# Two attention layers on one core: other engines for the matrix sums between the phases, and own timetables for the first and last pairs

## The chip, the cores and the metric

The kernel runs on one core of a Trainium2 chip. A core has a matrix engine (TensorE, "PE" in the profile), three engines for elementwise work (VectorE or DVE, ScalarE or ACT, GpSimd or POOL) and SyncE (SP), which in this kernel only issues transfers (DMA). Every engine works through its own list of instructions strictly in order; semaphores make one wait for another. The metric is the time of one execution on the device in microseconds (us), the median of several runs.

## The reference

The input `x` has 128 graphs of 64 nodes with 768 features, in float32, and `adj` holds which nodes are joined. Two layers follow, each with a residual and a normalisation over the features. The first is a graph attention of 12 heads of 64 with a gate, the second an ordinary masked attention of 6 heads of 128.

```python
# layer 0
h = einsum('bnd,ade->bane', x, W);  th = tanh(h)
attn = einsum(th, w_src) + swapaxes(einsum(th, w_dst), 2, 3)
attn = softmax(where(adj, leaky(attn, 0.2), -999))
f = elu(einsum('banm,bame->bane', attn, h) + b)
g = sigmoid(x @ H_w.T + H_b)
x = layernorm(x + g * f + (1 - g) * x)
# layer 1
q, k, v = x @ Wq + bq, x @ Wk + bk, x @ Wv + bv          # 6 heads of 128
ctx = softmax(q k^T / sqrt(128) + where(adj, 0, -9e15)) v
x = layernorm(x + ctx @ Wf + bf)
```

## The kernel before

**Tiles and phases.** The 8192 rows are 64 tiles of 128 (two graphs each), 32 pairs of tiles and 16 quads of two pairs. Phase a runs layer 0 pair by pair, and the values v of layer 1 two pairs behind; it writes x after layer 0 (`x1_there`), its transposed blocks (`ops_there`) and v (`v_there`) to the chip's memory. Phase b runs layer 1 quad by quad: queries and keys of three heads at a time (`q_0_0`, `k_0_0`, `q_0_1`, ...), a slab of attention for these, and the output product of the quad before.

**Products by sums.** All large matrix products follow schemes with fewer multiplications (of the Strassen and Winograd kind): sums of blocks are formed first, the products of sums are computed on TensorE, and their results are added up on the other engines. `by_token` (L409) does the two tiles of a pair by two halves of the columns in 7 products of 3 matmuls of 128x384, called P1, P6, P5, P2, P7, P3, P4 in this order; a pair has three such runs, `hidden` (h), `gate` (g) and `value` (v). `by_feature` (L520) and `output` (L1230) have 15 products of two matmuls of 128x256. For these the weights need sums too: a matrix of 18 blocks of 128x256 becomes 15 operands, by 15 sums of blocks (L341 on POOL, or L378, the helper `plus`, on VectorE) and two negated blocks (L344, on ScalarE).

**The border.** Wq and Wk are loaded into the places of layer 0's matrices while the last pair is at work (L328, 18 loads each of half a block). The first queries and keys of quad 0, `q_0_0` and `k_0_0`, are computed by `plain` (L496) from the raw matrices, so that the sums are needed only for `q_0_1` and `k_0_1`. Before, wq's sums run on POOL and wk's on VectorE. `load_third` (L464) loads the operands of quad 0 and `sums_of_quad` (L474, on POOL) makes their sums. The order on TensorE is: h and g of the last pair (p = 31), value(29), plain q, value(30), plain k, value(31), then phase b with `q_0_1` and `k_0_1`.

**Attention of a tile in phase a.** `attend` has 33 small steps on all engines. Those that the texts below speak of: L755 multiplies tanh(h) by the target weights; SP stores the sums (L763) and loads them back, spread over all rows (`bc_e`, L766); L779 adds the mask to them; L805 and twice L378 (`qk`, `th_d`) make the scores; ScalarE takes the exponential (L814); L819 sorts the halves of each number for a transpose by DMA (L823); L826 puts the transposed weights into `bc_e`; 24 small matmuls make the means (`f_all`, L835); L847/L848 divide them, L857 to L865 make the gated sum, L879 normalises, L887 and L891 turn the rows into the blocks for layer 1. L775/L776 sum the sources, L740 loads the tile's rows of x.

**Reads of the products.** L626 (h, P1, on ScalarE), L630, L633, L641, L645, L649 read h's products from PSUM; L670 to L686 those of the gate, L703 to L723 those of v, all in the `dense` buffers of six banks: a product waits until the one six before it has been read.

**Who decides the order.** A planner (`Beat`) writes each engine's list. Its clock counts beats: one beat is one product of `by_token`, a pair has 21. Every step of `attend` is put at the beat `begin + key` of a table: `FIRST_KEYS` for pairs 0 and 1, `KEYS` for all others, one row for each of the two tiles of a pair. Within a beat the earlier key goes first. The table moves nothing on the chip by itself; it decides what stands before what on each engine. All transfers stand in one list on SP, in the order in which the planner comes to them, and each waits for the eighth before it to have landed. `beat.start(line, after)` begins a chain of steps `after + 0.7` beats from now. In phase b the chain `slab` (s_ps, L1080; L1091 to L1105 on VectorE; c_ps, L1151) starts 0.25 beats after the keys; the reads of the output product (L1243, into `y`) are on VectorE too.

Of the kernel before, what the change touches and what calls it, by code (L numbers as in the profile page):

```python
# [49 lines left out]
ALU = mybir.AluOpType  # L50
# [115 lines left out]
FIRST_KEYS = (  # L166
    (
        (
            7.30, 8.42, 11.50, 8.19, 12.19, 14.50, 14.76, 14.89, 11.54, 17.99, 15.15,
            15.17, 15.52, 18.41, 19.39, 21.69, 23.72, 26.15, 26.31, 27.17, 27.75, 28.71,  # L170
            29.26, 30.33, 33.18, 34.13, 35.27, 35.86, 39.11, 15.41, 21.02, 22.80, 9.19,
        ),
        (
            8.80, 9.00, 13.78, 11.92, 12.01, 15.72, 15.83, 15.87, 13.82, 23.32, 19.70,
            20.58, 21.10, 23.37, 24.39, 24.67, 27.57, 29.73, 30.19, 32.26, 32.47, 32.59,
            33.08, 33.10, 34.28, 35.83, 36.62, 36.84, 39.74, 14.57, 15.41, 22.26, 5.31,
        ),
    ),
    (
        (  # L180
            7.11, 7.74, 9.44, 11.47, 13.51, 13.72, 14.07, 14.80, 16.89, 20.73, 14.98,
            16.33, 17.32, 18.31, 18.71, 20.99, 23.30, 25.33, 26.19, 26.22, 27.77, 27.77,
            28.33, 28.46, 28.97, 30.32, 34.83, 35.25, 39.50, 14.82, 25.50, 27.55, 9.19,
        ),
        (
            9.59, 9.73, 12.30, 13.34, 15.30, 17.56, 18.57, 18.68, 19.34, 24.26, 19.97,
            20.09, 21.15, 22.78, 23.21, 23.90, 26.80, 29.76, 30.49, 31.63, 32.60, 32.89,
            33.74, 34.77, 35.36, 36.41, 36.90, 37.00, 38.50, 16.23, 18.47, 20.43, 5.31,
        ),
    ),  # L190
)

SUMS = (42.40, 42.75, 43.18)
X_BLOCKS = (14.97, 20.25, 20.39)
MASKS = 7.19


FIRST_X_BLOCKS = {1: (2.01, 18.22, 19.86), 2: (17.02, 30.55, 37.15)}
GATE_SUMS = (4.29, 5.74, 7.17, 10.09)
ONE_MORE, VALUE_SUMS = 7.66, 21.30  # L200


class Beat:
# [46 lines left out]
def two_layers(  # L250
# [21 lines left out]
    nc = tc.nc  # L272
    n_tiles = x.shape[0] // P
    n_quads = n_tiles // 4
    n_pairs = n_tiles // 2
    beat = Beat()
# [42 lines left out]
    def thirds(w, name, engine, gap, blocks):  # L319

        t = fifteen(name)
        for k in range(3):
            for m in range(3):
                to = t[:, 3 * k + m]
                if len(blocks.shape) == 6:
                    to = to.rearrange("p c (r e) -> p c r e", r=2)
                    for c in range(2):
                        nc.sync.dma_start(to[:, c], blocks[k, m][:, c])  # L328
                        yield gap
                else:  # L330
                    nc.sync.dma_start(to, blocks[k, m])
                    yield gap
        ready[f"{name}_raw"] = t
        yield 3
        while not ready.get(f"{name}_used", True):
            yield 1
        for to, a, b, op in W_SUMS:
            if engine is nc.vector:
                plus(t[:, to], t[:, a], t[:, b], op)
            else:  # L340
                engine.tensor_tensor(t[:, to], t[:, a], t[:, b], op)  # L341
            yield gap
        for to in NEGATED:
            nc.scalar.mul(t[:, to], t[:, to], -1.0)  # L344
            yield gap
        ready[f"{name}_sb"] = t

# [5 lines left out]
    def by_head(w, name, engine, gap):  # L353

        yield from thirds(w, name, engine, gap, w.rearrange("(k c p) (r n e) -> k n p c r e", k=3, c=2, r=2, n=3))
# [97 lines left out]
    ready, dense = {}, []  # L453
# [90 lines left out]
    def phase_a(pa, ps_a, dst_pool):  # L544
# [67 lines left out]
        def hidden(p, A, B):  # L612
            u = {}

            def h_of(S, m):
                return S["h"][:, 6 * m : 6 * m + 6, 0:E0]

            def th_of(S, m):
                return heads(S["th"][:, m * HALF : (m + 1) * HALF], 6)

            def half_done(S, m):
                beat.soon(lambda: nc.scalar.activation(th_of(S, m), h_of(S, m), AF.Tanh))

            def p1(ps):
                u[1] = part(f"h1_{p}")
                nc.scalar.copy(u[1], ps)  # L626

            def p6(ps):
                u[2] = part(f"h2_{p}")
                nc.vector.tensor_tensor(u[2], u[1], ps, ALU.add)  # L630

            def p2(ps):
                nc.scalar.copy(h_of(A, 0), heads(ps, 6))  # L633
                nc.scalar.activation(th_of(A, 0), heads(ps, 6), AF.Tanh)

            def p5(ps):
                u[3] = part(f"h3_{p}")
                nc.vector.tensor_tensor(u[3], u[1], ps, ALU.add)

            def p7(ps):  # L640
                nc.vector.tensor_tensor(h_of(B, 1), heads(u[3], 6), heads(ps, 6), ALU.add)  # L641
                half_done(B, 1)

            def p4(ps):
                nc.vector.tensor_tensor(h_of(B, 0), heads(u[1], 6), heads(ps, 6), ALU.add)  # L645
                nc.scalar.activation(th_of(B, 0), h_of(B, 0), AF.Tanh)

            def p3(ps):
                nc.vector.tensor_tensor(h_of(A, 1), heads(u[2], 6), heads(ps, 6), ALU.add)  # L649
                nc.scalar.activation(th_of(A, 1), h_of(A, 1), AF.Tanh)  # L650

            by_token(f"h_{p}_", blocks[p], w0_sb, dict(P1=p1, P2=p2, P3=p3, P4=p4, P5=p5, P6=p6, P7=p7))


# [73 lines left out]
        def attend(S, begin):  # L728
            t, p, side, h, th = S["t"], S["p"], S["side"], S["h"], S["th"]
# [166 lines left out]
                means, divided, below, unit, gated, summed, measured, power_of, normal, part_rows,  # L896
                turn_rows, rows, tanh_of_gate, rest_of_gate, rest_of_x, rows_in,
            ]
            for step, key in zip(steps, (FIRST_KEYS[p] if p < 2 else KEYS)[side]):
                beat.at(begin + key, step)  # L900


        def sums_of_pair(p, begin):
            xo, so = x1_at(p), x1_sums
            b = [xo[:, i] for i in range(4)]
            x1_blocks[p] = b + [so[:, i] for i in range(4)]

            def first():
                plus(so[:, 0], b[2], b[3])
                plus(so[:, 1], so[:, 0], b[0], ALU.subtract)  # L910

            def last():
                nc.gpsimd.tensor_tensor(so[:, 2], b[0], b[2], ALU.subtract)
                nc.gpsimd.tensor_tensor(so[:, 3], b[1], so[:, 1], ALU.subtract)

            def away():
                there = ops_there[p // 2][:, p % 2].rearrange("p m c t -> p (m c) t")
                nc.sync.dma_start(there, xo.rearrange("p k c t -> p (k c) t"))

            for work, key in zip((first, last, away), SUMS):  # L920
                beat.at(begin + key, work)

        x1_blocks = {}
# [23 lines left out]
        def first_blocks():  # L947
            for k in (3, 4, 5, 0, 1, 2):
                load_third(0, f"A{k}")
                yield 8 if k == 5 else 0.5  # L950

        period = 3 * len(TURNS)
        for p in range(n_pairs):
            ta, tb = tiles_of(p)
            A = {"t": ta, "p": p, "side": 0}
            B = {"t": tb, "p": p, "side": 1}
            begin = p * period
            for side, S in enumerate((A, B)):
                S.update(h=h_of_tile[(2 * p + side) % 3], th=th_d[side], g=gates[side])
            masks(p, A, B, begin)  # L960
            for S in (A, B):
                attend(S, begin)
            sums_of_pair(p, begin)
            if p + 1 < n_pairs:
                line = x_blocks(p + 1)
                for key in [k - begin for k in FIRST_X_BLOCKS.get(p + 1, ())] or X_BLOCKS:
                    beat.at(begin + key, lambda line=line: next(line, None))
            beat.until(lambda: beat.now == begin)
            if p + 1 == n_pairs:
                ready["wq_used"] = ready["wk_used"] = False  # L970
                beat.start(first_blocks(), 4)
                beat.start(by_head(wq, "wq", nc.gpsimd, 0.3), 7)
                beat.start(by_head(wk, "wk", nc.vector, 0.5), 18)
                beat.start(sums_of_quad(0), 21)
            hidden(p, A, B)
            gate(p, A, B)
            blocks.pop(p)
            if p > 1:
                value(p - 2)
# [1 line left out]
        raw = quads[0].setdefault("raw", set())  # L981
        beat.until(lambda: "wq_raw" in ready and len(raw) == 6)
        plain("q_0_0_", ready["wq_raw"], 0, bq_sb, qk[:, 0])
        ready["wq_used"] = True
        value(n_pairs - 2)
        beat.until(lambda: "wk_raw" in ready)
        plain("k_0_0_", ready["wk_raw"], 0, bk_sb, qk[:, 1])
        ready["wk_used"] = ready["raw_used"] = True
        beat.until(lambda: beat.now > begin + SUMS[1])
        value(n_pairs - 1)  # L990
        beat.drain()

# [12 lines left out]
    def phase_b(pb, ps_b):  # L1005
# [263 lines left out]
        for q in range(n_quads):  # L1269
# [17 lines left out]
                beat.start(operands(before, 1), 6 if final else 0)  # L1287
            beat.until(lambda: "wk_sb" in ready)
            keys(q, 1, None if final else (lambda name: load_third(q + 1, name)))
            beat.start(slab(Q, 1), 0.25)  # L1290
            if final:
                beat.start(rows_of(Q, 0))
                give(0)
# [65 lines left out]
```

## Time and profile before

| what | value |
|---|---|
| median of 3 runs | 2843.06 us (2843.0 to 2844.84) |
| the profiled execution | 2841.36 us |
| its span, from first to last instruction | 2839.6 us |
| TensorE busy | 2777.5 us, 98% of the span |
| VectorE, ScalarE, GpSimd busy | 74%, 49%, 46% |
| mean granted TensorE clock | 0.996 of full speed |
| TensorE busy from 0 to 100 us | 74.51 us |
| TensorE busy from 1300 to 1400, 1400 to 1500 us | 93.21, 95.13 us |

The profile is one execution. Its parts give each engine's busy time, the longest groups of instructions by line of the kernel (L409 is line 409), and for each engine the waits: on which line it waited, for how long in all, how often, and the longest. Lines of the timeline begin with the start in us and the length; a bracket at the end holds the time the engine stood idle before and what released it. Phase a takes the time up to about 1446 us, phase b the rest.

### The profile page before, as it was taken

How to read it: one execution, taken by the hardware profiler on the slowest of the kernel's cores; microseconds unless marked ns; L12 is line 12 of the kernel's file. 1: busy time of each engine (PE TensorE's matmuls, PEld its weight loads, DVE VectorE, ACT ScalarE, POOL GpSimd, SP SyncE). 2: the span in 40 equal slices, each digit the busy share in tenths (PEclk: the TensorE clock that was granted, in tenths of full speed). 3: DMA queues.
4: the chain of work that ended last, by engine and by line, in shares of the span. 5: the costliest groups of instructions: out<-in, count | busy, mean ns of one | idle time of the engine just before them, and what ended most of it. 6: DMA issues, size and time to landing. Idle time of an engine off the chain costs nothing.

```text
span 2839.6 us, 43938 instructions
## 1 busy us (share of the span) xinstructions
PE 2777.5 (98%) x16002; PEld 2001.9 (71%) x16002; DVE 2111.3 (74%) x4182; ACT 1379.1 (49%) x1725; POOL 1316.8 (46%) x1119
## 2 busy tenths in 40 slices
PE   7899999999999999999899999999999999999998
PEld 4455555555555555555577888888888888888887
DVE  7888988988988888888645666756657656667556
ACT  2655656556656656656435344343443343443442
POOL 6656656656656656656724233312333212333123
PEclk9999999999999999999999999999999999999999
DMA  6566655656656656656654343343443443434432
GB/s 207 146 153 152 171 150 156 171 143 160 171 142 163 171 141 165 165 144 177 169 139 102 79 118 92 99 118 84 101 117 86 106 105 86 118 88 103 118 88 69
DMA packets 583688, 371.47 MB, mean 131 GB/s; under 512 B 435760, under 2 KB 533808, under 8 KB 583472
## 3 DMA queue, kind: packets, MB, share of 16 engines
q1 hardware_dynamic: 583472, 368.66, 51.0%
q8 instruction: 127, 2.08, 0.3%
q14 instruction: 89, 0.73, 0.1%
HBM read 167.81 MB, written 101.06 MB: 95 GB/s over the span
## 4 chain that ended last, share of the span: by engine, by line
PE 87%; DVE 5%; issue 2%; POOL 1%; DMA 1%; ACT 0%; SPq 0%; DVEq 0%; POOLq 0%; ACTq 0%
PE v L409 15%; PE h L409 14%; PE g L409 14%; PE k L520 13%; PE o L1230 13%; PE q L520 12%; PE f_all L835 2%; PE c_ps L1151 2%; PE s_ps L1080 2%; DVE s L1096 1%; DVE qk L534 1%; POOL zone L474 1%; DVE sc L378 1%; PE k L496 1%; DVE y L1243 1%
## 5 line engine op out<-in xcount | busy, mean ns | idle before, releaser
L409 PE MATMUL h<-w,zone 128*128 128x384 f32 x1320 | 446.0, 494 | 22.0 <-ACT h L626 12.9
L409 PE MATMUL g<-w,zone 128*128 128x384 f32 x1320 | 440.7, 489 | 3.9 <-DVE gate L680 3.0
L520 PE MATMUL q<-zone,w 128*128 128x256 f32 x1860 | 420.8, 382 | 5.9 <-DVE qk L534 3.3
L520 PE MATMUL k<-zone,w 128*128 128x256 f32 x1860 | 414.3, 382 | 2.8 <-DVE qk L534 2.8
L520 PEld LDWEIGHTS q<-zone,w 128*128 128x128 f32 x1860 | 349.5, 190 | 63.4 <-DVE qk L534 10.2
L520 PEld LDWEIGHTS k<-zone,w 128*128 128x128 f32 x1860 | 350.2, 190 | 58.9 <-DVE qk L534 8.3
L409 PEld LDWEIGHTS h<-w,zone 128*128 128x128 f32 x1320 | 251.1, 192 | 194.4 <-ACT h L626 14.1
L409 PEld LDWEIGHTS g<-w,zone 128*128 128x128 f32 x1320 | 248.2, 190 | 174.6 <-DVE gate L680 11.3
L433 POOL TENSOR_TENSOR rs<-rs,power 128x1 f32<-128x1 f32 x128 | 72.7, 568 | 627.0 <-DVE rs L431 623.3
L1230 PE MATMUL o<-w,sc 128*128 128x256 f32 x1320 | 317.0, 384 | 8.5 <-DVE y L1243 5.3
L474 POOL TENSOR_TENSOR zone<-zone 128x512 f32<-128x512 f32 x176 | 246.9, 1428 | 142.5 <-DMA zone<-ops_there 131.7
L1213 POOL TENSOR_TENSOR y<-y,bf_sb 128x768 f32<-128x768 f32 x62 | 113.6, 1852 | 383.2 <-DMA y<-x_there 366.6
L1230 PEld LDWEIGHTS o<-w,sc 128*128 128x128 f32 x1320 | 245.6, 190 | 54.2 <-DVE y L1243 15.6
L534 DVE TENSOR_TENSOR qk<-qk,k 128x256 f32<-128x256 f32 x310 | 127.4, 419 | 207.5 <-PE k L520 203.4
L1243 DVE TENSOR_TENSOR y<-y,o 128x256 f32<-128x256 f32 x496 | 195.6, 414 | 106.2 <-PE o L1230 102.5
L409 PE MATMUL v<-w,x_sums 128*128 128x384 f32 x768 | 259.3, 488 | 0.5 <-DVE v L707 0.3
L534 DVE TENSOR_TENSOR qk<-qk,q 128x256 f32<-128x256 f32 x310 | 125.7, 418 | 127.8 <-PE q L520 102.5
L409 PEld LDWEIGHTS v<-w,x_sums 128*128 128x128 f32 x768 | 146.2, 191 | 102.8 <-issue 2.2
L755 POOL TENSOR_TENSOR bc_e<-qk 128x768 f32<-128x768 f32 x32 | 61.9, 1936 | 273.7 <-ACT qk L650 273.7
L1162 ACT COPY parts<-c_ps 128x768 uint16<-128x768 uint16 x124 | 97.1, 796 | 187.2 <-PE c_ps L1151 177.9
L538 ACT ACTIVATE qk<-q,bq_sb 128x256 f32<-128x256 f32 x186 | 86.2, 471 | 177.1 <-PE q L520 112.2
L538 ACT ACTIVATE qk<-k,bk_sb 128x256 f32<-128x256 f32 x186 | 88.3, 475 | 106.7 <-PE k L520 106.6
(186 smaller groups left out, 4943.3 us busy)
## 6 DMA issues: line engine op xcount, KB each, us to landing
zone<-in_xT SPq DMA_DIRECT2D x32, 768.0 KB, 6.7
zone<-in_x SPq DMA_DIRECT2D x64, 384.0 KB, 3.8
bc_e<-there SPq DMA_DIRECT2D x128, 192.0 KB, 3.5
x_there<-mix SPq DMA_DIRECT2D x64, 384.0 KB, 4.2
v_there<-v SPq DMA_DIRECT2D x128, 192.0 KB, 2.4
zone<-ops_there SPq DMA_DIRECT2D x192, 128.0 KB, 2.5
v<-v_there SPq DMA_DIRECT2D x128, 192.0 KB, 4.3
y<-x_there SPq DMA_DIRECT2D x62, 384.0 KB, 4.7
```

What stands on the lines that cost most here:

```text
L409: nc.tensor.matmul(ps, lhsT=blocks[xb][:, c, :], rhs=w[:, wb, c, :], start=(c == 0 and to not in begun), stop=(c == KH - 1), skip_group_ch ...
L433: nc.gpsimd.tensor_tensor(rs[:, 0:1], rs[:, 0:1], power, ALU.pow)
L474: nc.gpsimd.tensor_tensor(to, a, b, op)
L520: nc.tensor.matmul(ps, lhsT=w[:, wb, c, r * P : (r + 1) * P], rhs=operand(xb)[:, c].rearrange("p i t -> p (i t)"), start=(c == 0 and not b ...
L534: nc.vector.tensor_tensor(part_of, part_of, ps, ALU.add if sign > 0 else ALU.subtract)
L538: nc.scalar.activation(part_of, ps, AF.Identity, bias=bias, scale=float(sign))
L755: nc.gpsimd.tensor_tensor(bc, th, w_dst_sb, ALU.mult)
L835: nc.tensor.matmul(f_all[b * N : (b + 1) * N, at : at + E0 + 1], lhsT=e[rows, hd // 2 * P + b * N : hd // 2 * P + (b + 1) * N], rhs=(h[row ...
L1162: nc.scalar.copy(of[:, i], halves(c_ps[i].rearrange("p n t -> p (n t)")))
L1213: nc.gpsimd.tensor_tensor(y, y, bf_sb, ALU.add)
L1230: nc.tensor.matmul(ps, lhsT=of[xb][:, c, :], rhs=wf_sb[:, wb, c, :], start=(c == 0 and not begun), stop=(c == 1), skip_group_check=True,)
L1243: nc.vector.tensor_tensor(part_of, part_of, ps, ALU.add if sign > 0 else ALU.subtract)
```

## The change

- `LAST_KEYS`: the last pair has a table of its own, and `LAST_SUMS` of its own for the sums of its blocks. The tables of pairs 0 and 1 have other values; `KEYS`, for pairs 2 to 30, is as it was.
- The beats at which the x blocks of pairs 1 and 2 are loaded and summed (`FIRST_X_BLOCKS`), and at which the sums of the gate's matrix and of Wv are made (`GATE_SUMS`, `VALUE_SUMS`, `ONE_MORE`), have other values.
- At the border, wq's sums are made by VectorE and wk's by POOL, with spacings of 0.23 and 0.89 beats. The two negated blocks are made by the same engine as the sums, not by ScalarE. The sums of wq may begin at beat 39.7 of the last pair, rather than where plain q has been written. The beats at which loads and sums begin stand in `BORDER`.
- In phase b the second slab of each quad but the first starts 1 beat after the keys rather than 0.25.
- `BY_VECTOR` is empty: L626 stays on ScalarE.

```diff
 FIRST_KEYS = (
     (
         (
-            7.30, 8.42, 11.50, 8.19, 12.19, 14.50, 14.76, 14.89, 11.54, 17.99, 15.15,
-            15.17, 15.52, 18.41, 19.39, 21.69, 23.72, 26.15, 26.31, 27.17, 27.75, 28.71,
-            29.26, 30.33, 33.18, 34.13, 35.27, 35.86, 39.11, 15.41, 21.02, 22.80, 9.19,
+            8.04, 8.42, 11.55, 8.19, 12.69, 14.50, 14.76, 14.90, 11.54, 18.77, 15.15,
+            15.17, 15.52, 18.16, 19.39, 21.69, 23.31, 25.96, 26.12, 27.36, 27.56, 28.52,
+            29.07, 30.14, 32.37, 34.03, 34.46, 35.05, 37.99, 15.73, 20.89, 22.80, 11.96,
         ),
...
+LAST_KEYS = (
+    (
+        7.34, 7.49, 12.22, 8.24, 8.88, 14.60, 15.07, 16.06, 15.31, 16.83, 16.55,
+        16.61, 16.79, 16.94, 17.18, 19.09, 22.37, 24.78, 26.19, 26.40, 27.56, 27.66,
+        28.66, 29.10, 30.61, 31.88, 33.49, 34.49, 37.52, 14.16, 16.26, 18.81, 10.03,
+    ),
+    (
+        8.84, 11.28, 14.41, 9.41, 18.23, 19.94, 19.99, 20.22, 15.08, 20.24, 20.63,
+        22.73, 22.88, 23.94, 24.79, 25.85, 27.49, 29.12, 29.88, 32.71, 32.97, 34.00,
+        35.06, 35.49, 36.55, 37.20, 37.40, 38.26, 38.99, 14.62, 20.51, 21.97, 5.34,
+    ),
+)
 SUMS = (42.40, 42.75, 43.18)
+LAST_SUMS = (42.40, 42.47, 45.11)
-FIRST_X_BLOCKS = {1: (2.01, 18.22, 19.86), 2: (17.02, 30.55, 37.15)}
-GATE_SUMS = (4.29, 5.74, 7.17, 10.09)
-ONE_MORE, VALUE_SUMS = 7.66, 21.30
+BY_VECTOR = ()
+BORDER = {
+    "first": 6.38,
+    "then": 10.79,
+    "wq": 6.93,
+    "wq_gap": 0.23,
+    "wk": 16.02,
+    "wk_gap": 0.89,
+    "wq_sums": 39.7,
+    "sums": 28.78,
+}
+FIRST_X_BLOCKS = {1: (1.83, 16.48, 19.32), 2: (15.83, 29.95, 41.68)}
+GATE_SUMS = (3.85, 5.19, 6.46, 8.04)
+ONE_MORE, VALUE_SUMS = 8.20, 21.04
...
         for to in NEGATED:
-            nc.scalar.mul(t[:, to], t[:, to], -1.0)
+            engine.tensor_scalar(t[:, to], t[:, to], -1.0, None, ALU.mult)
...
-            for step, key in zip(steps, (FIRST_KEYS[p] if p < 2 else KEYS)[side]):
+            for step, key in zip(steps, (LAST_KEYS if p + 1 == n_pairs else FIRST_KEYS[p] if p < 2 else KEYS)[side]):
                 beat.at(begin + key, step)
...
-            for work, key in zip((first, last, away), SUMS):
+            for work, key in zip((first, last, away), LAST_SUMS if p + 1 == n_pairs else SUMS):
                 beat.at(begin + key, work)
...
-                yield 8 if k == 5 else 0.5
+                yield BORDER["then"] if k == 5 else 0.5
...
-                beat.start(first_blocks(), 4)
-                beat.start(by_head(wq, "wq", nc.gpsimd, 0.3), 7)
-                beat.start(by_head(wk, "wk", nc.vector, 0.5), 18)
-                beat.start(sums_of_quad(0), 21)
+                beat.start(first_blocks(), BORDER["first"])
+                beat.start(by_head(wq, "wq", nc.vector, BORDER["wq_gap"]), BORDER["wq"])
+                beat.start(by_head(wk, "wk", nc.gpsimd, BORDER["wk_gap"]), BORDER["wk"])
+                beat.at(begin + BORDER["wq_sums"], lambda: ready.update(wq_used=True))
+                beat.start(sums_of_quad(0), BORDER["sums"])
...
-        ready["wq_used"] = True
         value(n_pairs - 2)
...
-        beat.until(lambda: beat.now > begin + SUMS[1])
+        beat.until(lambda: beat.now > begin + LAST_SUMS[1])
         value(n_pairs - 1)
...
-            beat.start(slab(Q, 1), 0.25)
+            beat.start(slab(Q, 1), 1 if before else 0.25)
```

## The prediction

> **What bounds the kernel now.** I read the totals of the page first, then 100 us windows, then TensorE's waits by line, then the timelines of the stretches that the waits point to.
>
> ```profile
> PE 2777.5 (98%) x16002; PEld 2001.9 (71%) x16002; DVE 2111.3 (74%) x4182; ACT 1379.1 (49%) x1725; POOL 1316.8 (46%) x1119
> ```
>
> TensorE is busy 98% of the span; the change alters none of its work, so only its gaps can move. The windows show where these are: 74.51 us busy of 0 to 100, all 100.00 of each window from 200 to 1300, and 95.13 of 1400 to 1500. The list of waits names them:
>
> ```profile
> PE h L409 <- ACT h L626: 12.9, 2, 6.9
> ...
> PE f_all L835 <- POOL w L341: 6.3, 1, 6.3
> PE o L1230 <- DVE y L1243: 5.9, 15, 0.6
> ...
> PE q L520 <- POOL zone L474: 2.4, 3, 1.1
> ...
> PE h L409 <- DVE h L641: 1.8, 1, 1.8
> PE f_all L835 <- ACT bc_e L826: 1.7, 1, 1.7
> ...
> PE v L409 <- DVE v L717: 1.1, 1, 1.1
> ```
>
> Columns: total us, times, longest. All gaps together are some 55 us. Two groups stand where the change works: the first pairs (L626, L641, L680, L670) and the border (L835, L717). TensorE's timeline gives their places and the slow stretch behind each:
>
> ```profile
> 50.19 3.58 PE L409 MATMUL h<-w,zone 128*128 128x384 f32 x6 [5.93 <-ACT h L626]
> 61.19 2.20 PE L409 MATMUL h<-w,zone 128*128 128x384 f32 x6 [1.81 <-DVE h L641]
> 77.87 2.20 PE L409 MATMUL g<-w,zone 128*128 128x384 f32 x6 [1.82 <-DVE gate L680]
> 92.82 6.38 PE L409 MATMUL h<-w,zone 128*128 128x384 f32 x12 [6.94 <-ACT h L626]
> ```
>
> The 6.3 us at the border is put down to POOL's L341. ScalarE's and SP's timelines say otherwise: L826, which writes the weights that f_all reads, ended at 1401.54, 0.1 us before TensorE resumed. It waited for a transpose that SP issued late:
>
> ```profile
> 1399.62 1.92 ACT L826 COPY bc_e<-th_d 128x1536 uint16<-128x1536 uint16 x1 [10.66 <-DMA th_d<-bc_e]
> ```
> ```profile
> 1391.70 3.83 SPq L328 DMA_DIRECT2D w<-in_wk  x6
> 1395.64 1.54 SPq L823 DMA_TRANSPOSE th_d<-bc_e  x1
> ```
>
> Its input was ready when L819 ended, at 1387.4; it stood 8.2 us behind wk loads of about 0.64 us each. So SP's queue, not the matrix sums, makes the largest border gap.
>
> [...]behind the 6.94 us gap twelve matmuls took 6.38 us, against 4.14 at 99.99. So a long gap costs 1.4 to 2.2 us beyond itself. [...]at 1431.69 four L378 weight sums took 5.43 us beside POOL, at 1439.79 four took 2.73. [...]
>
> **The change part by part.** Instructions per engine stay the same but for four negations (ScalarE to VectorE and POOL, two each). I took the order of each engine's instructions in the changed program and pushed the durations of this trace through it by hand.
>
> *Start (tables of pairs 0 and 1, gate sums, x blocks).* As places on the clock of before, gains carried on:
> - The second x-row load goes behind the bc_e loads of the first tile on SP: 0.8 + 0.5 us sooner, so L779 starts at about 36.6 (38.40). L680 moves ahead of L775/L776: the 0.98 gap at 36.25 goes. L626 ends at 48.3 (50.1): gain 1.8, but its gap stays about 5.3 us.
> - f_all of the first tile goes one product earlier and its L826 ahead of the other tile's L814 (0.85); L641 then has no softmax step ahead of it: the 1.81 gap goes. The h product of 61.19 starts at 57.4: gain 3.8.
> - L680 falls behind L775/L776 of the second tile and f_all of that tile comes earlier with a gap of 1.2: the product of 77.87 starts at 75.4: gain 2.5.
> - In pair 2, L626 ends at about 89 (92.77), leaving a gap of 6.1: gain 3.4. L670 (0.89) and one L680 (0.17) are no longer behind L848, and f_all comes a product earlier: value(0) starts at 114.8 (120.5): gain 5.7.
>
> From 200 to 1300 TensorE has no gap that could give this back. Sum: -5.6 us, from both sides -8 to +1: at the high end L626, in order on ScalarE behind L814 and L819, stays where it was.
>
> *Border.* More L464 and wq loads precede the last pair's own transfers on SP: four issues of about 0.62 more ahead of the dst store of 1356.77, so its bc_e lands 2.5 later, L779 starts at 1366.1 (1363.6), and L707, though moved ahead of L805, ends later. value(29) waits and plain q starts at 1377.3 (1374.91): loss 2.4. Queued on L707 are L714, L717 and three TensorE products. Then L826 of the first tile goes ahead of three L505 (0.48 each): 1.67 gap gone, f_all at 1385.3 (1384.51): loss 0.8. The transpose of 1395.64 has 11 wk loads ahead of it, not 15: 4 x 0.64 = 2.6 sooner, 1393.0. L826, 3.98 behind it, starts at 1397.0, f_all, 2.02 behind that, at 1399.0 (1401.64): gain 2.6. [...]f_all took 1.6 there against 0.87 elsewhere, the next twelve matmuls 4.83 against 4.1, 1.4 in all. L378 of mix (1.83) moves behind L717: gap of 1.09 gone. plain k starts at 1411.9 (1417.03): gain 2.6 + 1.4 + 1.1 = 5.1, from both sides +1 (transposes no sooner) to -8 (value(29) doesn't wait).
>
> *The sums.* wq: 15 x 0.69 on VectorE, up to 1.36 beside POOL, and two negations, a form not in the trace, at 0.3 to 0.6 (L1052's 0.29 for half the columns, and twice that): 11 to 22 us, run where VectorE was idle 12.16 us (1417.8 to 1429.9), and done long before q_0_1 (1446 in before). Behind it in the queue stand value(30)'s reads. wk: on POOL behind plain k, with three L474 among them: 3 x 1.43 + 15 x 1.28 + 2 x 1.42 (L750's 2.136 for 768 columns, by columns) = 26.3; with the means under contention (1.44, 1.69, 1.9) up to 33. k_0_1 began 29.1 us after plain k's end (1432.7 to 1461.79), its first product with a sum later. So hidden behind value(31) and q_0_1, with 3 us to spare; without that cover up to 4 us. Here I take nothing. ScalarE's L344 waited on nobody's path: 9 us idle before it. L474's own waits of 1495 to 1501 (2.4) move along unchanged.
>
> *Slabs.* In 15 quads the slab's s_ps matmuls come a product (0.86 us) later, and VectorE reads two y parts (0.41 each, L1243) ahead of L1096 and the bias wait of L1052. Phase b shows 13 waits "o <- DVE y" of 4.8 us, 0.2 to 0.6 each; most should go. Queued behind the slab: the transposes and c_ps, on which no wait shows. I take -2.5, from -5 to +4 (a quarter us of new wait per quad).
>
> *Sum:* -5.6 - 5.1 - 2.5 = -13.2. The profiled execution took 2841.36 (span 2839.6 and 1.76 around it); it becomes 2828.2. The median of the runs shown is 1.70 higher, 2843.06; against that 2829.9 us. What a measurement can tell from no change is 0.2%, 5.7 us.
>
> **Rivals.**
> - *Only half arrives.* The start gaps move instead of closing (L626 still ends behind the softmax chain of the tile before), or value(29)'s new wait eats the border's gain. For it: both paths run through several engines in order, and I have one trace. Against: no gap follows that could be named as heir. Start -2.5, border -2.5, slabs -1: 2837, at the edge of what can be told.
> - *No difference.* SP's queue limits the border as before (later dst store costs what the transpose wins) and the start gives its 5.6 back in pair 2: 2841, within 0.2%.
> - *Slower: the wk sums on POOL come late.* POOL's sums wait for plain k to let go of the raw blocks[...]. If all take what the longest L341 took (1.98; median 1.275), 20 operations are 39.6 us, 10 beyond k_0_1's need; the next quad's L474, behind them on POOL, then cost about 7 more (three of 1.43 and their waits of 2.4), and slabs that come late 4: 10 + 7 + 4 - 5.6 - 5.1 = +10, 2853. It decides from a POOL mean of about 1.45 us; before had 1.405 for L341 with VectorE at work. Against: VectorE, rid of the wk sums, would be busy some 14 of the 40 us from 1420 (24.29 less about 10), and its L534, with one input in PSUM, showed no stretching (0.42).
>
> **How the numbers follow.** As worked out (2823 to 2835): 0.54; more than that, where the slabs give 5 and L626's gaps lose their slow stretch (2815 to 2823): 0.08; half (2835 to 2839): 0.15, of which 0.09 is faster by over 0.2%; no difference (2839 to 2846): 0.10; slower: 0.13. Faster 0.54 + 0.08 + 0.09 = 0.71; same 0.06 + 0.10 = 0.16; slower 0.13. The range 2820 to 2843 leaves out the slower case, half of the fourth and the lower half of the second, some 0.2 in all; the likeliest case's own range is 2823 to 2835.
>
> **What would show it.** Right: "f_all <- POOL w L341" of 6.3 gone or near 3; the waits on L641 and L670 gone; a new wait of value(29) on L707 near 2; L626's two gaps near 5.3 and 6.1; "o <- DVE y" under 2.5; the negation on POOL ended before k_0_1's first product; plain k some 10.7 us sooner on the span's clock. Wrong: a wait of k on L341 or of its negation, a wait over 3 us at plain q, or pair 2 starting no sooner than 91.

## The result, and the profile after

The changed kernel takes 2831.40 us (median of 6 runs, 2829.88 to 2832.71), the kernel before 2843.09 (6 runs, 2839.69 to 2846.98). The ratio is 0.9957, 95% interval 0.9944 to 0.997: 11.7 us less, where 13.2 were forecast (2829.9). Lines of the changed kernel stand 26 further down than those of before from L341 on: L626 is L652, L835 is L861, L1243 is L1269.

The profiled execution of the changed kernel took 2832.71 us, the slowest of its six; that of before 2841.36. So the two traces differ by less, 8.7 us of span, than the medians. TensorE's list of waits after (columns: total us, times, longest):

```profile
PE h L435 <- ACT h L652: 9.4, 2, 5.7
...
PE f_all L861 <- ACT bc_e L852: 4.0, 1, 4.0
PE o L1256 <- DVE zone L1269: 3.5, 1, 3.5
...
PE g L435 <- DVE gate L706: 2.7, 1, 2.7
PE v L435 <- DVE v L733: 2.5, 1, 2.5
PE q L546 <- POOL zone L500: 2.4, 3, 1.1
...
PE o L1256 <- DVE y L1269: 1.3, 3, 0.9
PE v L435 <- DVE f_all L801: 1.1, 1, 1.1
```

Gone are h on L641, g on L670, v on L717 and the first f_all on L826. The 15 waits on y have become 3. New are value(29)'s two waits (v on L733 and on f_all) and one of 1.0 us before the f_all at 92.45, and at the very end the wait on zone has grown from 1.1 to 3.5. Four places in the two traces say what each part brought:

| place | before, us | after, us | gained so far | by this part | forecast |
|---|---|---|---|---|---|
| copy of h's first product, last pair | 1333.4 | 1329.8 | 3.6 | start 3.6 | 5.6 |
| plain k begins | 1417.03 | 1411.33 | 5.7 | border 2.1 | 5.1 |
| keys of the last quad begin | 2753.20 | 2740.80 | 12.4 | slabs 6.7 | 2.5 |
| end of the span | 2839.6 | 2830.9 | 8.7 | tail -3.7 | 0 |

TensorE's timeline after, at the start and at the border:

```profile
48.60 4.05 PE L435 MATMUL h<-w,zone 128*128 128x384 f32 x6 [5.75 <-ACT h L652]
75.18 3.19 PE L435 MATMUL g<-w,zone 128*128 128x384 f32 x6 [2.66 <-DVE gate L706]
88.55 2.91 PE L435 MATMUL h<-w,zone 128*128 128x384 f32 x6 [3.67 <-ACT h L652]
1397.16 0.36 PE L861 MATMUL f_all<-h,bc_e 64*64 64x65 f32 x1 [3.97 <-ACT bc_e L852]
1398.67 5.09 PE L435 MATMUL v<-w,x_sums 128*128 128x384 f32 x12
```

SP's timeline after, around the transpose that f_all waits for, and POOL's, with the sums of wk:

```profile
1388.83 1.86 SPq L354 DMA_DIRECT2D w<-in_wk  x3
1390.80 2.01 SPq L849 DMA_TRANSPOSE th_d<-bc_e  x1
```
```profile
1430.30 17.92 POOL L367 TENSOR_TENSOR w<-w 128x512 f32<-128x512 f32 x14
1448.19 3.68 POOL L370 TENSOR_SCALAR w<-w 128x512 f32<-128x512 f32 x2
```

The transpose still leaves 6 us after its input was ready (L845 ended at 1384.75). The sums of wk end at 1451.87, 4.3 us before k_0_1 begins at 1456.19.

### The profile page after: what moved, and what is told of

Read it like the earlier page. It is cut to its first block, busy times and chain, and to the rows that moved or that the text cites. A ratio compares the mean times of both kernels' runs of the same rounds, so it can differ in the third digit from the quotient of the medians.

```text
span 2830.9 us, 43960 instructions
## 1 busy us (share of the span) xinstructions
PE 2778.2 (98%) x16002; PEld 2002.6 (71%) x16002; DVE 2101.0 (74%) x4184; ACT 1378.4 (49%) x1721; POOL 1318.0 (47%) x1121
## 4 chain that ended last, share of the span: by engine, by line
PE 88%; DVE 5%; issue 1%; DMA 1%; POOL 1%; ACT 1%; SPq 0%; DVEq 0%; POOLq 0%; ACTq 0%
PE v L435 14%; PE h L435 14%; PE o L1256 14%; PE g L435 14%; PE k L546 13%; PE q L546 12%; PE f_all L861 2%; PE c_ps L1177 2%; PE s_ps L1106 2%; DVE s L1122 1%; DVE qk L560 1%; DVE sc L404 1%; PE k L522 1%; POOL zone L500 0%; DVE y L1269 0%
## 5 line engine op out<-in xcount | busy, mean ns | idle before, releaser
L435 PEld LDWEIGHTS g<-w,zone 128*128 128x128 f32 x1320 | 248.1, 190 | 173.9 <-DVE gate L706 10.7
L1269 DVE TENSOR_TENSOR y<-y,o 128x256 f32<-128x256 f32 x496 | 198.7, 416 | 119.6 <-PE o L1256 113.2
L564 ACT ACTIVATE qk<-k,bk_sb 128x256 f32<-128x256 f32 x186 | 88.6, 476 | 159.8 <-PE k L546 159.6
L564 ACT ACTIVATE qk<-q,bq_sb 128x256 f32<-128x256 f32 x186 | 86.0, 472 | 164.9 <-PE q L546 100.5
```

The costliest lines, as they stand in the source:

```text
L435: nc.tensor.matmul(ps, lhsT=blocks[xb][:, c, :], rhs=w[:, wb, c, :], start=(c == 0 and to not in begun), stop=(c == KH - 1), skip_group_ch ...
L564: nc.scalar.activation(part_of, ps, AF.Identity, bias=bias, scale=float(sign))
L1269: nc.vector.tensor_tensor(part_of, part_of, ps, ALU.add if sign > 0 else ALU.subtract)
```

## The experiments

Times are medians; a ratio is to the kernel before on the same chip, with its 95% interval. Undoing each part in the changed kernel came first.

**The slabs at 0.25 beats again.**

```diff
-            beat.start(slab(Q, 1), 1 if before else 0.25)
+            beat.start(slab(Q, 1), 0.25)
```

> The changed kernel with the slabs of phase b begun at 0.25 beats again; all else as changed. My reading of the two traces: between 1600 and 2750 us the later slab saves 6.7 us (13 waits of the output product on L1243's y, 4.8 us, shrink to 2, 0.4 us; the rest in stretches too short to be listed), and costs 3.7 at the end (a wait of 3.5 on the reads into zone instead of 1.1, with a slow stretch behind it). So: about 13 waits on y of 4 to 5 us come back, the tail's wait falls to about 1.1, and the time is 2831.4 + 6.7 - 3.7 = 2834.4. Rival 1, the tail's wait has nothing to do with the slab (it comes with the other starts): the tail stays, 2838. Rival 2, the later slab did nothing and the waits on y went with the places of the first quads: 2831, with y waits still near 0.4.

Measured 2838.81 us, ratio 0.9983 (0.9976 to 0.9989): 7.4 more than the changed kernel. Between 1590 and 2780 us the waits on y are back:

```profile
PE o L1256 <- DVE y L1269: 5.6, 14, 1.0
```

The later slab is worth more than I had for it. The tail's wait on zone is 2.7 here, against 3.5 in the changed kernel and 1.1 before: so the slab's place makes some 0.9 us of it, and most of what it grew by has another cause.

**The last quad's slab alone at 0.25** (`1 if before and not final else 0.25`).

> The changed kernel, but the slab of the last quad begins at 0.25 beats as before, the 14 others at 1. If the later last slab makes the tail's wait of 3.5 us on the reads into zone, that wait is about 1.1 again and no slow stretch follows: 2831.4 - 3.7 = 2827.7. Rival: the wait comes from where POOL's addition of the bias to y happens to fall beside VectorE's sums, which shifts with every microsecond of the phase: the tail then waits 2 to 4 us still, and the time is 2830 to 2832.

Measured 2830.35 us, 0.9949 (0.9937 to 0.9962): close to the changed kernel, with the two intervals overlapping, and with 2.7 us of waiting on zone. The last quad's slab alone thus does what all slabs did in the run before: it takes 0.9 us from this wait, and the larger part stays, as the rival has it.

**The start as before** (`FIRST_KEYS`, `FIRST_X_BLOCKS`, `GATE_SUMS`, `ONE_MORE`, `VALUE_SUMS` of the kernel before).

> The changed kernel with the tables of pairs 0 and 1, the x blocks of pairs 1 and 2 and the sums of the gate's and the value's matrix of before. The copies of h's first product (L626) in the last pair began 3.5 us sooner in the changed kernel's trace than in before's: that is what the start gave. So 2831.4 + 3.5 = 2834.9, with TensorE busy near 74.5 us of the first 100. Rival (gains at the start are lost again at the border, where SP's queue sets the pace): below 2833.

Measured 2838.05 us, 0.9979 (0.997 to 0.9988): 6.7 more. The last pair's copy of h's first product is back at 1333.4, and the waits on L641 (1.8) and L670 (0.9) are back. I had expected 3.5 from one trace, which was a poor draw. Against the 1333.4 us of before, this copy starts 3.0 to 6.2 us sooner in the nine profiles with the new start (4.9 in the mean), and 0.0 to 2.0 us later in the three other ones with the old (0.7 in the mean): 5.6 us between the means, what was forecast.

**The border as before** (last pair's table and sums, engines, negation and beats of the kernel before).

> The changed kernel with everything of the border as before: the last pair's table and sums, the engines of wq's and wk's sums, ScalarE's negation, the beats of all loads. By the traces the border gave 5.7 - 3.6 = 2.1 us (plain k against the start's gain). So 2833.5, with f_all's wait near 6.3 again and value(29)'s two waits of 2.45 and 1.14 gone. Rival (what the border gives is worth more, since phase b's places depend on it): 2836 or more.

Measured 2833.93 us, 0.9963 (0.9951 to 0.9976): 2.5 more, as expected, but the interval overlaps that of the changed kernel, so the medians alone do not show it. f_all waits 6.4 again, value(29) 1.8 instead of 3.6. The profiles say something similar. From the copy of h's first product in the last pair to the start of plain k, the four with the old border took 82.6 to 84.5 us (83.6 in the mean) and the seven with the new one 80.4 to 83.8 (82.1): 1.5 us, and the two ranges overlap too.

**Only the engines of the sums as before.**

```diff
-            engine.tensor_scalar(t[:, to], t[:, to], -1.0, None, ALU.mult)
+            nc.scalar.mul(t[:, to], t[:, to], -1.0)
...
-                beat.start(by_head(wq, "wq", nc.vector, BORDER["wq_gap"]), BORDER["wq"])
-                beat.start(by_head(wk, "wk", nc.gpsimd, BORDER["wk_gap"]), BORDER["wk"])
+                beat.start(by_head(wq, "wq", nc.gpsimd, BORDER["wq_gap"]), BORDER["wq"])
+                beat.start(by_head(wk, "wk", nc.vector, BORDER["wk_gap"]), BORDER["wk"])
```

> The changed kernel with only the engines of the matrix sums as before (wq's on POOL, wk's on VectorE, both negations on ScalarE), all beats as changed. If the sums are hidden wherever they are made, nothing moves: 2831.4 within 1.5 us, and TensorE waits neither on the sums nor on the negations. Rival[...]: 1.5 to 3 us more, 2833 to 2834.5, with a wait of v or f_all longer than in the changed kernel.

Measured 2831.34 us, 0.9958 (0.9945 to 0.997): the same median as the changed kernel. f_all waits 4.0 in both. But in this trace the sums do hold somebody up (ScalarE's timeline, then TensorE's):

```profile
1431.73 1.15 ACT L370 ACTIVATE w<-w 128x512 f32<-128x512 f32 x2 [7.57 <-POOL w L367]
1432.79 0.46 ACT L531 ACTIVATE qk<-k,bk_sb 128x256 f32<-128x256 f32 x1
1433.14 0.47 ACT L729 COPY v<-v 128x384 f32<-128x384 f32 x1
```
```profile
1433.66 2.20 PE L435 MATMUL v<-w,x_last 128*128 128x384 f32 x6 [1.62 <-ACT v L729]
```

ScalarE's negations wait 7.57 us for POOL's sums of wq, the read of v (L729) stands behind them in its list, and TensorE waits 1.62 us in value(31). In the changed kernel no such wait exists. So what the part that the title names first can be seen to take away is this one wait, and the medians of six and five runs cannot tell even that.

**wk's loads behind the transpose.** The loads get a spacing of their own; the sums keep theirs.

```diff
-                        yield gap
+                        yield load
...
-                beat.start(by_head(wk, "wk", nc.gpsimd, BORDER["wk_gap"]), BORDER["wk"])
+                beat.start(by_head(wk, "wk", nc.gpsimd, BORDER["wk_gap"], 0.5), 25.3)
```

> The changed kernel, with the 18 loads of wk begun at beat 25.3 of the last pair instead of 16.02 and 0.5 beats apart, so that the transpose for the second tile's f_all (L849) stands ahead of all but one of them on SP. If SP's queue makes f_all's wait (4.0 us in the changed kernel's trace): the transpose goes out near 1385 instead of 1390.8, f_all does not wait over 0.5, no slow stretch follows, and plain k starts 4 to 5.5 us sooner: 2826 to 2827.5. Rival (ScalarE's or VectorE's own chain is as late as the queue): the wait stays over 2.5 and the time within 1.5 of 2831.4. Second rival (the loads are then late for plain k): plain k waits on the load of wk, and the time is above 2832.

Measured 2830.22 us, 0.9958 (0.9944 to 0.9972). The mechanism held; the gain is not clear of the spread. SP's timeline, and TensorE's at value(29), in this run:

```profile
1384.08 1.31 SPq L849 DMA_TRANSPOSE th_d<-bc_e  x1
1385.44 10.96 SPq L354 DMA_DIRECT2D w<-in_wk  x15
```
```profile
1365.91 3.13 PE L435 MATMUL v<-w,x_sums 128*128 128x384 f32 x6 [3.35 <-DVE v L733]
1370.27 3.92 PE L435 MATMUL v<-w,x_sums 128*128 128x384 f32 x6 [1.23 <-DVE f_all L801]
```

The transpose leaves 6.7 us sooner and f_all does not wait at all. But value(29) waits 3.35 us here instead of 2.45, and behind it two times six matmuls take 3.13 and 3.92 us instead of 2.17 each: 2.7 us lost in slow stretches. This loss is not the doing of the later loads. Of the nine profiles with the new table of the last pair, eight have a slow stretch at value(29), and only the changed kernel's has none (granted clock 1.00 from 1360 to 1376): its profile was a lucky one there. By the stretch from the copy of h's first product to plain k, the later loads bring some 3 us: 79.6 us here and 78.2 in the kernel with both parts mended below, against 82.1 in the mean of the seven without them.

**Is it SP's queue or L341?** The kernel before, with `ready["wq_used"] = True` moved behind `value(n_pairs - 2)`.

> The kernel before, with the sums of wq on POOL allowed only after value(30) is written, so that POOL's L341 comes behind the second tile's f_all; SP's order as it was. If SP's queue makes the 6.3 us wait of f_all that the profile puts down to L341: the wait stays between 5.5 and 7, under another name, and L826 still ends 0.1 us before f_all starts. Rival (L341 is the cause, as the profile has it): the wait falls below 2 and the span is 4 to 6 us shorter.

One execution: 2847.62 us. POOL's L341 now begins at 1416.12, 15 us after f_all, and f_all waits as long as ever, with nobody to put it down to; ScalarE's L826 ends 0.09 us before f_all begins (TensorE's timeline, then ScalarE's):

```profile
1401.33 0.34 PE L835 MATMUL f_all<-h,bc_e 64*64 64x65 f32 x1 [5.70 <-issue]
```
```profile
1399.34 1.90 ACT L826 COPY bc_e<-th_d 128x1536 uint16<-128x1536 uint16 x1 [10.31 <-DMA th_d<-bc_e]
```

The run before took SP's queue away and the wait went; this one took POOL's sums away and it stayed. Together they settle it: the 6.3 us that the profile named after POOL's sums were SP's queue. Why this kernel is some 4 us slower than before was not followed up; its waits on y are 8.8 us, not 5.9.

**The slabs at 1.75 beats** (`1.75 if before else 0.25`).

> The changed kernel with the second slab of a quad at 1.75 beats instead of 1. The slab at 0.25 cost 7 us against 1. If what counts is only that the reads into y come ahead of the slab's first sums on VectorE, nothing more is gained: 2831.4 within 1.5, waits on y under 1.5 us. If each product of delay gave its part: 2827 or less. If the slab's transposes and c_ps become late: waits of the output product on c_ps's copies or on the sums sc, 2833 or more.

Measured 2856.44 us, 1.0045 (1.0031 to 1.0059): 25 us over the changed kernel, and slower than before. A new wait takes the place of the old one in 14 quads (TensorE's waits, then ScalarE's timeline in one quad):

```profile
PE q L546 <- ACT qk L564: 19.0, 14, 1.4
```
```profile
2193.44 1.47 ACT L1158 COPY sT<-s 128x1536 uint16<-128x1536 uint16 x1 [4.78 <-DVE s L1131]
2194.82 1.20 ACT L564 ACTIVATE qk<-q,bq_sb 128x256 f32<-128x256 f32 x3
```

ScalarE waits 4.78 us for the slab's weights, and the reads of the next quad's queries (L564) stand behind that copy in its list; TensorE resumes at 2195.43 once they have freed its banks. Of the three places tried the one at 1 lies between two cliffs: 0.25 costs 7 us, 1.75 costs 25.

**The tail.** In the changed kernel POOL's and VectorE's timelines have, near the end:

```profile
2792.59 1.80 POOL L1239 TENSOR_TENSOR y<-y,bf_sb 128x768 f32<-128x768 f32 x1
```
```profile
2792.70 1.97 DVE L404 SCALAR_TENSOR_TENSOR sc<-sc,cT 128x256 f32<-128x256 f32 x1
```

POOL begins 0.11 us ahead, and VectorE's sum takes 1.97 us where it takes 0.42 alone (the expectation below counts two sums, 0.84; it is one). In the kernel before the same two instructions met the other way round (VectorE's timeline, then POOL's):

```profile
2804.76 0.42 DVE L378 SCALAR_TENSOR_TENSOR sc<-sc,cT 128x256 f32<-128x256 f32 x1
```
```profile
2804.88 1.98 POOL L1213 TENSOR_TENSOR y<-y,bf_sb 128x768 f32<-128x768 f32 x1 [0.19 <-issue]
```

VectorE's sum took 0.42, and the read into zone that TensorE waits for came 1.1 us after TensorE was ready, not 3.5. This meeting is not left to chance: in the traces of the changed kernel and of the six variants of it above, up to the later loads of wk, POOL is 0.11 to 0.12 us ahead; in all three traces of the program before (two of them variants) VectorE is 0.12 us ahead, and POOL has the same 0.19 us of idle time before its addition. The test puts POOL's addition ahead of its scale steps:

```diff
-                yield 1
+                yield 0.2 if q + 1 == n_quads and i == 1 else 1
```

> The changed kernel, with POOL's second addition of the bias to the last rows of y planned 0.2 beats behind the first instead of 1, so that it stands ahead of POOL's scale steps and is done before VectorE's last sums sc. In the changed kernel's trace this addition started 0.11 us before VectorE's sums and held them for 1.97 us instead of 0.84; in before's it started 0.12 us after and held nothing. If that is what makes the tail's wait of 3.5 us, it falls to 1.5 to 2.4 with less of a slow stretch: 2829 to 2830. Rival (the wait follows VectorE's longer list there[...]): still 3 us or more, 2831.4 within 1.

Measured 2830.08 us, 0.9953 (0.9941 to 0.9966). The wait is 2.1, and the four and eight matmuls behind it take 1.13 and 1.89 us instead of 1.99 and 2.76, so no slow stretch:

```profile
2792.30 1.13 PE L1256 MATMUL o<-w,sc 128*128 128x256 f32 x4 [2.14 <-DVE zone L1269]
```

In this trace, the fastest of its five runs, that is 1.4 us of wait and 1.7 of slow stretch; the medians differ by 1.3, less than their spread can tell.

**Both mended.**

> The changed kernel with the later loads of wk (which took f_all's wait away) and the earlier addition at the end (as in e9_tail_early). If both work and add up, 1.2 and 2: 2828 to 2829, and the fastest of all. If the tail keeps its wait: 2830.2.

Measured 2827.26 us, 0.9945 (0.9931 to 0.9958): the lowest median of all, with neither f_all's wait on L852 nor the long one at the end (2.4). Its interval overlaps that of the changed kernel, so that it is faster is likely but not shown.

**The later slab alone, in the kernel before.**

> The kernel before with the second slab of each quad but the first at 1 beat instead of 0.25, nothing else. Taking this out of the changed kernel cost 7.4 us. If it is worth the same without the other parts: 2843.6 - 7.4 = 2836.2, y's waits of the output product down from 5.9 to about 1. Rival (parts overlap: their removals sum to 16.5 us, the whole change to 12): it is worth 3 to 5 alone, 2838.5 to 2840.5.

Measured 2836.56 us, 0.9977 (0.9968 to 0.9986): 6.3 below the 2842.88 of before, with 0.8 us of waits on y. So the slab is worth 6 to 7 us with or without the other parts. It also completes the account of the tail. Here VectorE's sum takes 0.42 us, as in the kernel before, and yet the wait on zone is longer than there:

```profile
PE o L1230 <- DVE zone L1243: 2.0, 1, 2.0
```

The wait on zone in all traces but that of the slab at 1.75, by the two things that change it:

| last quad's slab | VectorE's sum 0.42 us | VectorE's sum 1.97 us |
|---|---|---|
| 0.25 beats after the keys | 1.1, 1.1 | 2.7, 2.7 |
| 1 beat after the keys | 2.0, 2.1, 2.4 | 3.5, 3.6, 3.6, 3.6, 3.9 |

The later slab adds some 0.9 us and the meeting with POOL some 1.5, each with or without the other.

## Why the prediction was right, and where its sizes were off

The time, the range and the sign held. The sum held better than its terms, and that was luck: the slabs gave some 4 us more than forecast, the border 3 us less, and a loss at the end that the forecast did not have took 3.7. One of the named signs failed, plain k "some 10.7 us sooner": it came 5.7 us sooner. The removals of the three parts sum to 16.6 us, more than the 11.7 of the whole change. The loss at the end stays, whole or for the larger part, in all three kernels with one part undone, so 3 to 3.7 of these 4.9 us are what one would expect; this was not tested apart.

- *Start, -5.6: right.* The removed waits are those named (0.98 of L680, L641, L670), and the size is 5.6 over the profiles. Single steps were off: before the gate product at 75.18 there is a gap of 2.66 with a slow stretch behind it (six matmuls in 3.19 us, against 2.20 in the kernel before); L626's second gap is 3.67, not 6.1, but f_all behind it waits 0.99 and ran at a granted clock of 0.50 (from 92 to 94 us; its 48 matmuls took 1.69 us, 0.93 before), which my steps did not have. The forecast gain of 5.7 at value(0) was 3.95 in this trace (116.55 for 120.50).
- *Border, -5.1: mechanism right, size 1.5 to 2.5, not clear of the spread.* Three terms were mis-sized. The 1.4 us were to be saved because a gap of 2.9 us would bring no slow stretch. That was my assumption; the trace of before, whose gaps were 1.82 us or less and 5.93 or more, did not show it. The gap was 3.97, f_all took 1.51 us and the next twelve matmuls 5.09 (granted clock 0.50 from 1398 to 1400), so none of the 1.4 was saved. In the run with the earlier addition at the end it was 2.70, and the same twelve still took 5.19. "4 x 0.64 = 2.6 sooner": against the last pair's own clock the transpose left 1.2 sooner (1390.80 + 3.6 against 1395.64). "value(29) waits, loss 2.4": it waited 2.45 + 1.14, less the 0.32 that it had waited before: 3.3, and in the eight other profiles with this table a slow stretch came on top. The wait on L717 and the first f_all's went as said.
- *The sums, nothing: right.* 3 L474 and 15 L341 at 1.27 to 1.28, the two negations at 1.84 instead of the estimated 1.42: 26.5 us against 26.3, done 4.3 us early. The rival of late sums did not come about. Swapping the engines back left the median where it was, though that trace has a wait of 1.62 us behind ScalarE's negations, which my terms did not have.
- *Slabs, -2.5: mechanism right, undersized.* VectorE reads y ahead of the slab's long steps, and 13 waits of 4.8 us became 2 of 0.4. I counted only half of them; and another 2.1 us is time that the trace counts as busy (my guess, not shown: stalls too short for the list): TensorE's busy time over nearly the same work (7308 matmuls from 1600 to 2750 us before, 7311 from 1593.2 to 2737.6 after) fell from 1140.14 to 1138.00, at a granted clock of 1.00 in both. Removing the shift costs 7.4, adding it alone gives 6.3.
- *Tail, 0: missed.* The wait on zone (1.13 to 3.55) and its slow stretch (1.7 over twelve matmuls, granted clock 0.50 from 2798 to 2800) are the 3.7 us at the end. Behind the slab the prediction saw only transposes and c_ps, "on which no wait shows"; in the last quad the reads into zone come later too, by 0.9 us. The other 1.5 us come from the meeting of two engines that start within 0.13 us of each other. With the slab at 1.75 the wait is 1.1 (VectorE's sum 0.42). By what path the slab delays these reads, and why POOL was 0.19 us slower to start in the program before (its profile names no cause), stays open.

The rival "only half arrives" had the border right: half or more of that gain did not come, and value(29)'s waits are part of the reason. The rival of late slabs was real but lies further on, between 1 and 1.75 beats.

## What to carry to other kernels

A wait that the profile puts on one engine may belong to a queue: look for the instruction that ended just before the wait did, and follow its own wait back to where the transfer was issued. When an order is tuned by hand or by tables, a step that comes too late can cost far more than its best place gains (here 25 us against 7), so keep away from the late side. And count stalls by the time the whole stretch takes, not only by the list of waits: here nearly a third of the slabs' gain was in time that no list of waits shows.

## What the runs showed of the hardware that I had not expected

- A slow stretch of TensorE came behind shorter gaps than I had assumed. In the traces of the kernels before and after, the granted clock falls to 0.50 eight times while TensorE still has work, for 3.41 us four times and for 6.83 us four times, and every time behind a gap of 2.66 us or more: 5.93, 6.94 and 6.29 before; 5.75, 2.66, 3.67, 3.97 and 3.55 after. Behind the other 16 gaps of over 0.9 us in the two traces (0.91 to 2.45) no such stretch begins.
- In between, the length of a gap alone does not decide. Before the same gate product of the start, gaps of 2.51 to 2.66 us brought a slow stretch in four traces, and gaps of 2.67 to 2.69 us none in five. The changed kernel's line at 75.18 above is one of the four (3.19 us for six matmuls, granted clock 0.56 and 0.58 over the next two 2 us windows). One of the five, from the run with the earlier addition at the end:

```profile
75.51 2.20 PE L435 MATMUL g<-w,zone 128*128 128x384 f32 x6 [2.69 <-DVE gate L706]
```

  In that same trace the gap of 2.70 us at the border did bring one (twelve matmuls in 5.19 us, 4.14 at 99.99 in the kernel before):

```profile
1396.92 5.19 PE L435 MATMUL v<-w,x_sums 128*128 128x384 f32 x12
```

  My estimate from these figures, for this kernel: a gap under 2 us mostly costs itself alone, one over 3.5 us (all seven in the two traces) brings a slow stretch, and in between it differs from one execution to the next.
- Which instruction is stretched turned on 0.1 us. With POOL's addition begun 0.11 us ahead, VectorE's sum took 1.97 us instead of 0.42 and ended 0.28 us behind the addition; with VectorE's sum begun 0.12 us ahead, it took 0.42, and POOL's addition 1.98 against a median of 1.81. Both outcomes occur with the instructions in the same order in the lists, but not by chance: all seven traces of the changed program and its variants up to the later loads of wk gave the one, all three of the program before the other.
- The gain of the same start varies by about 3 us between the profiles of the nine kernels that have it (3.0 to 6.2), while phase a behind it runs without a gap (TensorE is busy for all 1100 us from 200 to 1300 in the kernels before and after) and keeps the difference to the end. One profile is not enough to price a part of 3 us.
